# Moving the merging of norm statistics and small per-row operations from VectorE to GpSimd in a four-layer graph network kernel

## Chip, cores and metric

The kernel runs as one program on one NeuronCore of a Trainium2 chip. The metric is the device time of one execution in microseconds (us). The core has five engines with their own instruction queues, each served in order: PE (TensorE, matrix multiplication; PEld is its weight load), DVE (VectorE), ACT (ScalarE), POOL (GpSimd) and SP (SyncE, which here only issues DMAs). They meet through semaphores alone, so the order in each queue is fixed when the program is built.

## The reference

There are 32 graphs of 512 nodes with 64 features, with a weighted adjacency matrix (some 1.6% of the entries by chance, on a symmetric pattern, and all diagonals) and a node mask. Four layers follow each other, and each ends in a norm over the 64 features of a node:

```python
def _layernorm(x, axis=-1, eps=1e-5):
    m = jnp.mean(x, axis=axis, keepdims=True)
    v = jnp.var(x, axis=axis, keepdims=True)
    return (x - m) / jnp.sqrt(v + eps)

x = _layernorm(x + _L0_gnn_ref(x, adj), axis=-1)   # degree-normalised sum over neighbours
x = _layernorm(x + _L1_gnn_ref(x, adj, ...), axis=-1)   # Chebyshev polynomials of the Laplacian, 4 orders
x = _layernorm(x + _L2_gnn_ref(x, adj, ...), axis=-1)   # hyperbolic attention over all pairs of nodes
x = _layernorm(x + _L3_gnn_ref(x, adj, nodemask, ...), axis=-1)   # weighted quantiles over the neighbours, two dense layers
return x
```

Layer 2 forms for all pairs of nodes a logarithmic map, an attention weight and a weighted sum, and then an exponential map back. Layer 3 thins out the neighbours of busy nodes, sorts each feature over a node's neighbours and mixes the quartiles.

## The kernel before

A graph of 512 nodes is held as T = 4 tiles of 128 partitions, so a value for each node is a tile of 128x4 (`col`) and a feature matrix one of 128x256 (`wide`). For each of the 32 graphs (batches) five stages are written down, called lanes: *front* (load the adjacency blocks, transpose them, layers 0 and 1), *pairs* and *tail* (layer 2), *graph* (which neighbours remain, the order of the nodes, the slots), *gather* and *sort* (layer 3: one-hot matmuls bring neighbour features into slots, a network of max and min sorts them), and for every two batches *head* (the rest of layer 3, the dense layers and the last norm). The last two batches use the lane *ends* for some of head's work, and *check* tests the node degrees against the limits of the fast path. A dense path for other graphs stands behind a branch (`tc.If`) and isn't taken on these data.

None of this is issued in the order in which it is written. Class `Order` (lines 181 to 400) is a recorder: helpers such as `tt`, `ts`, `stt` (DVE, lines 447 to 455), `act` (ACT, 477), `gtt` and `gts` (POOL, 470 to 475) and `mm` (PE) don't issue but record an operation with its engine, an assumed issue time, an assumed further delay until its result can be read (tail), and what it reads and writes. `issue` (line 295) then plays all of it through on five assumed clocks. An operation becomes ready when what it depends on is done by these times (another engine's result costs HOP = 0.1 us more, DVE's a further 0.15). Of the ready operations of an engine, the one with the smallest due time is taken; a due time is a period of 80 us times the batch number plus a share between the two bounds that the table `STAGES` gives the lane (line 1415). On PE, an operation of another tile shape than the last is set back by `STAY` us (line 188). Gaps of PE that the recorder sees are filled with matmuls on zeros (`stay_active`, lines 1453 and 1454; 1081 of them), and a change between ACT's two tables of functions puts in a table load. The resulting order is then pinned for each engine.

So a recorded time does two things: it says where an operation comes in the order, and where its readers do. The time on the chip is another matter; an engine waits there for whatever its next instruction in order needs.

The norms are made by `layernorm` (line 725), four times a batch: two in front (on `z`, and on layer 1's sum in PSUM into `FL`), one in tail (into `x3`) and one in the dense part of head (in place on `zo`). Each takes four statistics on DVE (line 714: `bn_stats` leaves six columns for each tile, count, mean and variance times count, of the even and of the odd elements), merges them with four `bn_aggr` (line 717, into `mv`), adds epsilon (`var`, DVE), takes the power -0.5 on POOL (`rsqrt`, line 722), makes the offset -mean times that (`off`, DVE), and applies both on ACT. The second front norm's caller reads the variance again.

Other small operations that the change touches: in front the degree `deg` gives `dm`, its power `dsc` and a mask `pos` (all 128x4); in graph `order` copies the rank to `rkh`, which head reads much later; in tail `s1` is put together from two columns and a row sum. POOL also clears parts of the sort's buffers SB and SH (line 1157), for which it waits until the sort of an earlier batch has let go of them.

Of the kernel before, what the change touches and what calls it, by code (L numbers as in the profile page):

```python
# [8 lines left out]
F32 = mybir.dt.float32  # L9
# [11 lines left out]
P = 128  # L21
# [159 lines left out]
class Order:  # L181
# [3 lines left out]

    ENGINES = ("PE", "DVE", "ACT", "POOL", "SP")
    HOP = 0.1
    STAY = 51.0

    def __init__(self, nc, tc):  # L190
        self.nc, self.tc = nc, tc
# [212 lines left out]
def tile_adj_resnorm(ctx: ExitStack, tc: tile.TileContext, x, adj, nodemask, w1k, b1k, att_w, att_b,  # L404
# [42 lines left out]
    def tt(out, a, b, op):  # L447
        vec(lambda: nc.vector.tensor_tensor(out, a, b, op=op), out, [a, b])  # L448

    def ts(out, a, s1, s2, op0, op1=None):  # L450
        kw = {} if op1 is None else {"op1": op1}
        vec(lambda: nc.vector.tensor_scalar(out, a, s1, s2, op0=op0, **kw), out, [a], True, (s1, s2))  # L452
# [4 lines left out]
    def cp(out, a):  # L457
        vec(lambda: nc.vector.tensor_copy(out, a), out, [a], True)
# [6 lines left out]

    def gp(f, out, ins):

        seq.op("POOL", 1.0, 0.5, f, [out], ins)

    def gtt(out, a, b, op):  # L470
        gp(lambda: nc.gpsimd.tensor_tensor(out, a, b, op=op), out, [a, b])
# [247 lines left out]
    def rsqrt(v, name):  # L719

        y = col(name)
        seq.op("POOL", 0.8, 0.6, lambda: nc.gpsimd.tensor_tensor(y, v, mhalf, op=OP.pow), [y], [v])  # L722
        return y

    def layernorm(dst, z):

        st = seq.tile(pools["small"], [P, T, nc.vector.BN_STATS_DIM], F32, "st", 2)
        mv = seq.tile(pools["small"], [P, T, nc.vector.BN_AGGR_DIM], F32, "mv", 2)
        for t in range(T):
            bn_stats(st[:, t, :], z[:, t, :])  # L730
        for t in range(T):
            bn_aggr(mv[:, t, :], st[:, t, :])
        var = col("var")
        ts(var, mv[:, :, 1], EPS, None, op0=OP.add)
        rs = rsqrt(var, "rs")
        off = col("off")
        stt(off, mv[:, :, 0], -1.0, rs, op0=OP.mult, op1=OP.mult)
        for t in range(T):
            act(dst[:, t, :], z[:, t, :], AF.Identity, bias=off[:, t:t + 1], scale=rs[:, t:t + 1])
        return mv[:, :, 1], rs  # L740
# [89 lines left out]
    def order(b, res):  # L830

        gm = pools["gm"]
        V = res["V"]
        key = col("key")
        stt(key, M3[:, b, :], float(N), iotr, op0=OP.mult, op1=OP.add)
        pt = bank()
        for t in range(T):
            tr(pt[:, t * P:(t + 1) * P], key[:, t:t + 1].to_broadcast([P, P]), identf)
        keyh = col("keyh")
        ts(keyh, key, -0.5, None, op0=OP.add)  # L840
        sg = col("sg")
        for t in range(T):
            junk = seq.tile(gm, [P, N], F16, "junk", 1)
            act(junk, pt, AF.Sign, bias=keyh[:, t:t + 1], scale=-1.0, accum_out=sg[:, t:t + 1])
        rk = col("rk")
        ts(rk, sg, -0.5, 0.5 * N - 1.0, op0=OP.mult, op1=OP.add)

        rkh = seq.tile(pools["keep"], [P, T], F16, "rkh", 8)
        cp(rkh, rk)
        perm = seq.tile(gm, [P, T, N], F16, "perm", 1, "nbT")  # L850
        for t in range(T):
            ts(perm[:, t, :], iotap, rk[:, t:t + 1], None, op0=OP.is_equal)
        VP = seq.tile(gm, [P, T, N], F16, "VP", 1, "v")
        for j in range(T):
            pt = bank()
            for t in range(T):
                mm(pt, V[:, t, j * P:(j + 1) * P], perm[:, t, :], start=(t == 0), stop=(t == T - 1))
            act(VP[:, j, :], pt, AF.Copy)
        slot = seq.tile(pools["keep"], [P, T, N], F16, "slot", 2)
        for j in range(T):  # L860
            pt = bank()
            for k in range(j + 1):
                mm(pt, UC[:, :P] if k == j else UC[:, P:2 * P], VP[:, k, :], start=(k == 0), stop=(k == j))
            act(slot[:, j, :], pt, AF.Copy)
        pt = bank()
        for k in range(T):
            mm(pt, onesP, VP[:, k, :], start=(k == 0), stop=(k == T - 1))
        if b % 2 == 0:
            res["ohm"] = OHM[:, b // 2 % 3]
        dist = seq.tile(gm, [P, H2], F16, "dist")  # L870
        for i in range(P // HM):
            hm, h = slice(i * HM, (i + 1) * HM), i % 2
            act(dist[hm], pt[hm, h * H2:(h + 1) * H2], AF.Abs, bias=npart[hm])
        for i, hm in enumerate((PADS, RANKS)):
            act(res["ohm"][hm, i, b % 2, :], dist[hm], AF.Relu, bias=1.0, scale=-1.0)
        res["slots"] = slot, rkh
# [5 lines left out]
    def front(b, res):  # L882

        A, xa = load(b)
        mid = pools["mid"]
        AT = transposed(A)
        res["AT"] = AT

        def amul(rhs, n):

            pt = bank()[:, :T * n].rearrange("p (t n) -> p t n", n=n)
            for t in range(T):
                for j in range(T):
                    mm(pt[:, t, :], AT[:, j, t * P:(t + 1) * P], rhs[:, j, :],
                                     start=(j == 0), stop=(j == T - 1))
            return pt

        def amul_halves(y):

            pt = bank()  # L900
            for j in range(2):
                for h in range(2):
                    mm(pt[h * D:(h + 1) * D, :], y[:, 2 * h + j, :], AT[:, 2 * h + j, :], start=(j == 0), stop=(j == 1), pair=True)
            sums = seq.tile(mid, [P, N], F32, "sums", 1)
            act(sums, pt, AF.Copy)
            pt = bank()[:, :T * D].rearrange("p (t n) -> p t n", n=D)
            for t in range(T):
                mm(pt[:, t, :], sums[:, t * P:(t + 1) * P], fold, start=True, stop=True)
            return pt


        pt = amul(xa, D + 1)
        deg = col("deg")
        cp(deg, pt[:, :, D])
        dc = col("dc")
        ts(dc, deg, 1.0, None, op0=OP.max)
        recip(dc, dc)
        z = wide("z")
        tt(z, pt[:, :, :D], bc(dc), op=OP.mult)
        tt(z, z, xa[:, :, :D], op=OP.add)  # L920
        R = seq.tile(mid, [P, T, KO * D], F32, "R", 1)
        layernorm(R[:, :, :D], z)


        dm = col("dm")
        ts(dm, deg, 2e-35, None, op0=OP.max)
        dsc = rsqrt(dm, "dsc")
        pos = col("pos")
        ts(pos, deg, 0.0, None, op0=OP.is_gt)
        tt(dsc, dsc, pos, op=OP.mult)  # L930
        g = col("g")
        ts(g, deg, 0.0, None, op0=OP.not_equal)
        for k in range(1, KO):
            prev = R[:, :, (k - 1) * D:k * D]
            y = wide("y")
            tt(y, prev, bc(dsc), op=OP.mult)
            pt = amul_halves(y)
            q = wide("q", "y")
            tt(q, pt, bc(dsc), op=OP.mult)
            cur = R[:, :, k * D:(k + 1) * D]  # L940
            if k == 1:
                pg = wide("pg", "z")
                tt(pg, prev, bc(g), op=OP.mult)
                prev = pg
            tt(cur, prev, q, op=OP.subtract)
        RT = seq.tile(mid, [P, KO * D // P, N], F32, "RT", 1)
        for u in range(KO * D // P):
            pt = bank()
            for t in range(T):
                tr(pt[:, t * P:(t + 1) * P], R[:, t, u * P:(u + 1) * P], identf)  # L950
            act(RT[:, u, :], pt, AF.Copy)
        pt = bank()[:, :T * (D + 2)].rearrange("p (t n) -> p t n", n=D + 2)
        nu = KO * D // P
        for t in range(T):
            mm(pt[:, t, :], onesb, bias1, start=True, stop=False)
            for u in range(nu):
                mm(pt[:, t, :], RT[:, u, t * P:(t + 1) * P], wk[:, u, :], start=False, stop=(u == nu - 1))

        FL = FLS[:, b % 2]
        var, rs = layernorm(FL[:, :, :D], pt[:, :, :D])  # L960
        tt(FL[:, :, D + 2:D + 7:4], pt[:, :, D:], bc(rs, 2), op=OP.mult)

        w2 = col("w2")
        stt(w2, var, float(D), rs, op0=OP.mult, op1=OP.mult)
        tt(FL[:, :, D:D + 34:33], bc(w2, 2), bc(rs, 2), op=OP.mult)
        ts(FL[:, :, D + 3:D + 36:32], bc(FL[:, :, D], 2), -1.0, 1.0, op0=OP.mult, op1=OP.add)
        res["FL"] = FL

    def pairs(b, res):
# [126 lines left out]
        s1 = col("s1")  # L1096
        gtt(s1, SS[:, :, D], SS[:, :, D + 1], op=OP.add)
        q = rowsum(x2, S, "xs")
        stt(s1, q, -2.0, s1, op0=OP.mult, op1=OP.add)
        tt(s1, s1, hh, op=OP.mult)  # L1100
        u = wide("u")
        tt(u, S, bc(hb), op=OP.mult)
        v = wide("v")
# [280 lines left out]
    def within_bounds():  # L1384
# [17 lines left out]
        for i, op in enumerate((OP.is_gt, OP.is_lt)):  # L1402
# [9 lines left out]

    STAGES = {"front": (-0.6, -0.5), "pairs": (1.2, 1.3), "tail": (0.2, 1.5), "graph": (0.9, 1.0), "gather": (2.7, 2.9),
              "sort": (4.5, 4.6), "head": (4.7, 5.6), "ends": (4.0, 4.5), "check": (3.4, 4.8)}

    nc.scalar.preload_act_table_set("natural_log_exp_and_others")
    with ExitStack() as fast:
# [285 lines left out]
```

## Time and profile before

| What | Value |
|---|---|
| Runs | 2621.48, 2621.71, 2628.53 us, median 2621.71 |
| The profiled execution | 2622.02 us, its span 2620.2 us, mean granted PE clock 0.982 |
| Busy, DVE / PE / ACT / POOL | 2402.7 / 2458.2 / 1879.2 / 815.8 us |
| Largest DVE groups | SB products (sort) 565.8 us, SH products 347.4 us, one-hots `oh` 252.3 us |
| The power on POOL, front norms | 64 times, mean 1303 ns, 83.4 us |
| Aggregations `bn_aggr` | front 256 times, 33.5 us; head 128, 11.7 us; tail 128, 11.5 us |
| DMA | 49.96 MB in the span, mean 19 GB/s |

The span goes from the first to the last instruction of the profiled execution. A group is named by the program's tiles, output <- inputs, with the lane ahead (`tail_mv<-tail_st`), and its shapes. Busy time is the time in which at least one instruction of the group or engine ran; instructions of DVE overlap with the next one, so that 128 aggregations of 148 ns (median) are busy for 11.5 us only. A wait is the time in which an engine's next instruction stood idle, with the instruction that released it. In the timeline a line gives the start in us from the span's start, the length, and how many like it follow each other. The slices of the page are 65.5 us long.

### The profile page before, as it was taken

To read this page: it belongs to the slowest core of one execution; us is meant where nothing else is said; L and a number is where in the kernel's file an instruction comes from. 1 tells how busy PE (TensorE), PEld (TensorE's weight loads), DVE (VectorE), ACT (ScalarE), POOL (GpSimd) and SP (SyncE) were. 2 spreads that over 40 slices of the span, in tenths; PEclk is the share of its full clock that TensorE was granted. 3 is DMA by queue.
4 is the path that set the end of the run, shared out by engine and by line. 5 is a ranking of instruction groups with operands and counts; after the bars stand their busy time and mean duration, and the time that the engine had idled before them with its cause. 6 is when DMAs were issued, how large, how long until landed. Compare 5 with 4: busy or idle time off the path is not lost.

```text
span 2620.2 us, 55667 instructions
## 1 busy us (share of the span) xinstructions
PE 2458.2 (94%) x19641; PEld 1635.4 (62%) x19667; DVE 2402.7 (92%) x9002; ACT 1879.2 (72%) x4406; POOL 815.8 (31%) x1783
## 2 busy tenths in 40 slices
PE   7999999999999999999999999999999999999997
PEld 6666566666666666666656666566666666666655
DVE  3668998999999999999999999999999999998996
ACT  5666677767777777767777677777777778776761
POOL 1233332332343333322333233333323333332210
PEclk9999999999999999999999899999999999998999
DMA  1100000000000000000000000000000000000000
GB/s 38 33 23 21 17 14 15 25 22 23 18 11 22 20 25 21 24 17 13 20 21 25 19 19 13 20 23 22 26 19 13 18 19 26 19 11 3 5 7 8
DMA packets 119723, 49.96 MB, mean 19 GB/s; under 512 B 53740, under 2 KB 119436, under 8 KB 119436
## 3 DMA queue, kind: packets, MB, share of 16 engines
q1 hardware_dynamic: 118272, 46.15, 6.4%
q8 instruction: 156, 2.56, 0.4%
q14 instruction: 131, 1.07, 0.1%
q10 hardware_dynamic: 1164, 0.18, 0.0%
HBM read 37.93 MB, written 8.39 MB: 18 GB/s over the span
## 4 chain that ended last, share of the span: by engine, by line
DVE 72%; PE 18%; ACT 6%; issue 2%; POOL 2%; DMA 0%; ACTq 0%; DVEq 0%
DVE SB L448 17%; DVE SH L448 8%; DVE gather_oh L452 6%; PE front_bank L502 5%; DVE pairs_Q L448 4%; PE gather_bank L502 3%; PE graph_bank L502 3%; DVE pairs_RW L448 3%; PE pairs_bank L502 3%; DVE sort_prod L448 3%; DVE pairs_Wt L455 3%; DVE pairs_L L455 2%; DVE tail_v L448 2%; DVE pairs_EX L448 2%; DVE pairs_RW L455 2%
## 5 line engine op out<-in xcount | busy, mean ns | idle before, releaser
L448 DVE TENSOR_TENSOR SB<-SB 128x448 f32<-128x448 f32 (+11 forms) x1424 | 565.8, 424 | 12.2 <-ACT SB L483 0.7
L502 PE MATMUL gather_bank<-gather_oh,tail_x3h 128*64 128x448 f16 (+5 forms) x5376 | 516.5, 321 | 4.8 <-ACT SB L483 3.4
L502 PEld LDWEIGHTS <-tail_x3h 128*64 128x64 bf16 x5376 | 296.0, 111 | 214.3 <-issue 112.8
L448 DVE TENSOR_TENSOR SH<-SH 128x32 f32<-128x32 f32 (+11 forms) x1744 | 347.4, 246 | 8.1
L502 PE MATMUL pairs_bank<-pairs_FT 67*128 67x512 f32 (+7 forms) x768 | 316.9, 516 | 18.7 <-ACT pairs_EX L483 7.1
L452 DVE TENSOR_SCALAR gather_oh<-graph_slot 128x256 f16<-128x256 f16 (+9 forms) x864 | 252.3, 337 | 25.3 <-PE gather_bank L502 23.5
L502 PE MATMUL front_bank<-front_AT,front_y 128*64 128x512 f32 x768 | 189.5, 607 | 18.5 <-DVE front_y L448 17.0
L502 PEld LDWEIGHTS pairs_bank<-pairs_FT 67*128 67x128 f32 (+1 forms) x768 | 130.2, 194 | 83.2 <-issue 19.7
L502 PE MATMUL graph_bank<-graph_perm,graph_V 128*128 128x512 f16 x512 | 141.0, 382 | 16.1 <-DVE graph_perm L452 13.8
L502 PEld LDWEIGHTS <-graph_nbT 128*128 128x128 f16 x1536 | 113.1, 99 | 57.6 <-issue 17.3
L722 POOL TENSOR_TENSOR front_rs<-front_var,mhalf 128x4 f32<-128x4 f32 x64 | 83.4, 1303 | 201.8 <-DVE front_var L452 152.9
L502 PEld LDWEIGHTS front_bank<-XA,front_AT 128*128 128x128 f32 x1024 | 126.0, 194 | 13.6 <-issue 6.3
L1453 PE MATMUL PA<-zero 128*128 128x256 bf16 x973 | 132.9, 278 | 0.1
L502 PE MATMUL pairs_bank<-FLS,pairs_Wt 128*128 128x66 f32 x1024 | 124.7, 274 | 3.9 <-DVE pairs_Wt L455 3.8
L502 PEld LDWEIGHTS pairs_bank<-FLS,pairs_Wt 128*128 128x128 f32 x1024 | 120.6, 192 | 10.9 <-DVE pairs_Wt L455 7.8
L502 PE MATMUL front_bank<-XA,front_AT 128*128 128x65 f32 x1024 | 124.5, 274 | 0.0
L448 DVE TENSOR_TENSOR pairs_RW<-pairs_RW,pairs_EX 128x640 f32<-128x640 f32 x128 | 104.1, 815 | 18.7 <-ACT pairs_RW L483 18.4
L502 PEld LDWEIGHTS <-tabs 128*128 128x128 f16 x1296 | 78.3, 100 | 64.2 <-issue 54.9
L502 PEld LDWEIGHTS front_bank<-front_AT,front_y 128*64 128x64 f32 x768 | 54.5, 137 | 95.6 <-issue 63.0
L483 ACT ACTIVATE graph_VP<-graph_bank 128x512 f16<-128x512 f32 x128 | 75.5, 590 | 53.7 <-PE graph_bank L502 49.4
L483 ACT ACTIVATE SB<-gather_bank 128x448 f32<-128x448 f32 (+2 forms) x192 | 81.3, 438 | 43.4 <-PE gather_bank L502 43.0
L502 PE MATMUL head_bank<-head_PT,sort_ap 128*64 128x512 f32 x240 | 111.2, 608 | 0.1
(354 smaller groups left out, 6569.8 us busy)
## 6 DMA issues: line engine op xcount, KB each, us to landing
front_A<-in_adj_dram SPq DMA_DIRECT2D x128, 256.0 KB, 2.7
XA<-in_x_dram SPq DMA_DIRECT2D x32, 128.0 KB, 2.2
xs<-tail_x SPq DMA_DIRECT2D x32, 128.0 KB, 1.9
out_dram<-head_zo SPq DMA_DIRECT2D x31, 128.0 KB, 2.0
out_dram<-tail_ends SPq DMA_DIRECT2D x1, 128.0 KB, 2.1
wk<-in_L_gnn_weight_dram ACTq DMA_DIRECT2D x1, 64.0 KB, 3.0
w1s<-in_L_gnn_W_dram ACTq DMA_DIRECT2D x2, 32.0 KB, 2.0
attw<-in_L_gnn_att_W_dram ACTq DMA_DIRECT2D x2, 0.2 KB, 3.2
```

Of the source, the lines that this page charges most:

```text
L448: vec(lambda: nc.vector.tensor_tensor(out, a, b, op=op), out, [a, b])
L452: vec(lambda: nc.vector.tensor_scalar(out, a, s1, s2, op0=op0, **kw), out, [a], True, (s1, s2))
L455: vec(lambda: nc.vector.scalar_tensor_tensor(out, a, s, b, op0=op0, op1=op1), out, [a, b], False, (s,))
L483: 0.3, lambda: nc.scalar.activation(out, a, f, scale=scale, **kw), [out, accum_out], [a, after] + sc, table)
L502: return nc.tensor.matmul(out, w, a, start=start, stop=stop)
L722: seq.op("POOL", 0.8, 0.6, lambda: nc.gpsimd.tensor_tensor(y, v, mhalf, op=OP.pow), [y], [v])
L1453: return nc.tensor.matmul(PA[:, 2 * P:], zero[:, :P], zero, start=False, stop=False)
```

## The change

- `layernorm` gets a parameter `soon`. The two front norms pass True and stay as they were. For the two others (tail and head) the merging of the statistics is written out for POOL: the mean of the means, the squared half difference of the means, the sum of the variances divided by 64, the power, and the offset. The statistics themselves stay on DVE and the last step on ACT.
- Six further operations on 128x4 move from DVE to POOL: `dm`, `pos` and the product with `dsc` in front, the copy `rkh` in graph, and in tail the two steps on `s1` (which become three).
- The recorder's assumed times for POOL go from 1.0 + 0.5 us to 0.28 + 0.25 for a small operation and from 0.8 + 0.6 to 1.1 + 0.3 for the power; `STAY` goes from 51 to 49, and in `STAGES` the bounds of tail, graph, gather, ends and check are altered. These four change the order on every engine.

```diff
-    STAY = 51.0
+    STAY = 49.0
...
-        seq.op("POOL", 1.0, 0.5, f, [out], ins)
+        seq.op("POOL", 0.28, 0.25, f, [out], ins)
...
-        seq.op("POOL", 0.8, 0.6, lambda: nc.gpsimd.tensor_tensor(y, v, mhalf, op=OP.pow), [y], [v])
+        seq.op("POOL", 1.1, 0.3, lambda: nc.gpsimd.tensor_tensor(y, v, mhalf, op=OP.pow), [y], [v])
...
-    def layernorm(dst, z):
+    def layernorm(dst, z, soon=False):
+
+        if not soon:
+
+            st = seq.tile(pools["small"], [P, T, nc.vector.BN_STATS_DIM], F32, "st", 2)
+            for t in range(T):
+                bn_stats(st[:, t, :], z[:, t, :])
+            off, even, var, d, odd, v = (st[:, :, i] for i in range(6))
+            gtt(d, even, odd, op=OP.subtract)
+            gtt(var, var, v, op=OP.add)
+            gts(d, d, 0.5, None, op0=OP.mult)
+            gts(var, var, 1.0 / D, EPS, op0=OP.mult, op1=OP.add)
+            gtt(d, d, d, op=OP.mult)
+            gtt(v, var, d, op=OP.add)
+            rs = rsqrt(v, "rs")
+            gtt(off, even, odd, op=OP.add)
+            gts(off, off, -0.5, None, op0=OP.mult)
+            gtt(off, off, rs, op=OP.mult)
+            for t in range(T):
+                act(dst[:, t, :], z[:, t, :], AF.Identity, bias=off[:, t:t + 1], scale=rs[:, t:t + 1])
+            return
...
-        cp(rkh, rk)
+        gts(rkh, rk, 1.0, None, op0=OP.mult)
...
-        layernorm(R[:, :, :D], z)
+        layernorm(R[:, :, :D], z, True)
...
-        ts(dm, deg, 2e-35, None, op0=OP.max)
+        gts(dm, deg, 2e-35, None, op0=OP.max)
         dsc = rsqrt(dm, "dsc")
         pos = col("pos")
-        ts(pos, deg, 0.0, None, op0=OP.is_gt)
-        tt(dsc, dsc, pos, op=OP.mult)
+        gts(pos, deg, 0.0, None, op0=OP.is_gt)
+        gtt(dsc, dsc, pos, op=OP.mult)
...
-        var, rs = layernorm(FL[:, :, :D], pt[:, :, :D])
+        var, rs = layernorm(FL[:, :, :D], pt[:, :, :D], True)
...
-        stt(s1, q, -2.0, s1, op0=OP.mult, op1=OP.add)
-        tt(s1, s1, hh, op=OP.mult)
+        gts(q, q, -2.0, None, op0=OP.mult)
+        gtt(s1, s1, q, op=OP.add)
+        gtt(s1, s1, hh, op=OP.mult)
...
-    STAGES = {"front": (-0.6, -0.5), "pairs": (1.2, 1.3), "tail": (0.2, 1.5), "graph": (0.9, 1.0), "gather": (2.7, 2.9),
-              "sort": (4.5, 4.6), "head": (4.7, 5.6), "ends": (4.0, 4.5), "check": (3.4, 4.8)}
+    STAGES = {"front": (-0.6, -0.5), "pairs": (1.2, 1.3), "tail": (0.7, 1.2), "graph": (1.2, 1.3), "gather": (2.7, 3.1),
+              "sort": (4.5, 4.6), "head": (4.7, 5.6), "ends": (4.3, 4.4), "check": (3.4, 4.7)}
```

## The prediction

> **What bounds the kernel now.** I read the page first, then the busy time by stretches, then DVE's waits, then DVE's timeline inside one batch. From the page:
>
> ```profile
> PE 2458.2 (94%) x19641; PEld 1635.4 (62%) x19667; DVE 2402.7 (92%) x9002; ACT 1879.2 (72%) x4406; POOL 815.8 (31%) x1783
> DVE  3668998999999999999999999999999999998996
> DVE 72%; PE 18%; ACT 6%; issue 2%; POOL 2%; DMA 0%; ACTq 0%; DVEq 0%
> ```
>
> DVE is busy 92% of the span, in slices four to thirty-nine nearly always, and 72% of the chain that ended last is DVE. PE's 94% is no proof of a bound, since its matmul ends are modelled and it holds filler matmuls (line 1453). POOL, the engine that takes the work over, is busy 31%.
>
> The steady stretch, first all engines, then the fillers alone (columns: stretch, length, busy time of PE, PEld, DVE, ACT, POOL, PE clock, DMA share, GB/s; in the second line only PE and PEld):
>
> ```profile
> 656.00:2296.00 1640.00, 1558.03 (x12419) 1025.93 (x12436) 1569.64 (x5852) 1237.58 (x2905) 548.38 (x1135) 0.99 0.07 20
> ```
>
> ```profile
> 656.00:2296.00 1640.00, 22.26 (x138) 12.88 (x138) 0.99 0.07 20
> ```
>
> DVE is busy 95.7% here, and PE without the fillers 1558.0 - 22.3 = 1535.8 us, 93.6%. So DVE is the tighter of two engines that are nearly level. DVE idles 70 us here, of which its waits on PE and ACT for operands are most; its waits on POOL in the whole run are:
>
> ```profile
> DVE head_off L455 <- POOL head_rs L722: 4.0, 5, 1.1
> DVE front_off L455 <- POOL front_rs L722: 3.4, 5, 0.9
> DVE tail_off L455 <- POOL tail_rs L722: 1.7, 3, 0.9
> ```
>
> (us in total, number of times, longest). 9.1 us over 128 places (64 + 32 + 32): 0.07 us a place. That matters below, because these three are the places where the recorder's old time for POOL (0.8 + 0.6 us for the power, line 722) was already close to the measured 1.3 to 1.5 us.
>
> **What the change takes off DVE.** Per batch: two norms (tail and head) lose four aggregations, one variance and one offset each (12 instructions); six more go to POOL (dm, pos, the product with dsc, the copy rkh, two on s1). That is 18 of 128x4 or less, 576 over 32 batches; the built lists agree. What one is worth is read from the timeline, as the distance to the next start and not as its length, since neighbours overlap:
>
> ```profile
> 1379.38 0.36 DVE L717 BATCH_NORM_AGGREGATE head_mv<-head_st 128x2 f32<-128x6 f32 x4
> 1379.66 0.19 DVE L452 TENSOR_SCALAR gather_oh<-graph_slot 128x256 f16<-128x256 f16 x1
> 1379.78 0.17 DVE L452 TENSOR_SCALAR head_var<-head_mv 128x4 f32<-128x4 f32 x1
> 1379.86 0.49 DVE L452 TENSOR_SCALAR gather_oh<-graph_slot 128x256 f16<-128x256 f16 x3
> ...
> 1384.23 0.15 DVE L455 SCALAR_TENSOR_TENSOR tail_off<-tail_mv,tail_rs 128x4 f32<-128x4 f32 x1
> 1384.31 1.08 DVE L448 TENSOR_TENSOR SB<-SB 128x896 f32<-128x896 f32 x1
> ```
>
> Four aggregations hold DVE for 0.28 us, a variance for 0.08, an offset for 0.08. So two norms: 2 x (0.28 + 0.08 + 0.08) = 0.88 us. The other six at the same 0.07 (dm at 1425.09, pos at 1425.16, the next at 1425.23; rkh at 1413.72, the next at 1413.80): 0.42. Together 1.3 us a batch, **-41 us** over 32. If each counted its busy time in the group rows, it would be 11.7 + 11.5 for the aggregations and some 50 for the ten others, 73 us: the far end. The near end is zero, if DVE only idles longer. I take -41, because the starts are what a full queue is made of.
>
> The two offsets also take their waits off DVE: 4.0 + 1.7, **-6 us**.
>
> **What it adds.** POOL gets 25 instructions a batch (9 for each of two norms, 3 for dsc, 1 for rkh, 3 for s1), 800 in all. Rows of the same shape take 0.25 to 0.45 us in most groups (tail_al<-tail_xy 247 ns, pairs_sq 461 ns): some 270 us, so POOL goes from 816 to about 1090 us, 42%. Hidden beside DVE, if its answers come in time. Where are they awaited? The power that it delays is no longer followed by DVE in tail and head but by ACT, which has 28% idle. On DVE there are six places a batch that read a POOL answer and that the recorder used to plan too late (1.0 + 0.5 us an operation) and now plans at 0.28 + 0.25: two reciprocals, the products with s1, al, y2 and rnr. Planned closely, a place costs what the three above cost: 6 x 32 x 0.07 = **+14 us**. Bounds: zero (nothing late), and for the far end the row with the widest spread: tail_nr 769 ns, the power 1421, tail_rnr 762, 2.95 us in sequence against 0.53 + 1.4 + 0.53 = 2.46 now planned, 0.5 us late, 6 x 32 x 0.5 = 96 us.
>
> POOL is served in order, and a fill of SB (line 1157) waits there for DVE:
>
> ```profile
> POOL SB L1157 <- DVE SB L448: 263.6, 65, 17.9
> ```
>
> 65 waits, up to 17.9 us. Behind a fill the built order has a power of the front norm 26 times (18 before), and the new s1 steps 12 times. A front power that stands there is late for DVE's front_off. The row front_off (3.4 us) is what 18 such places cost in the worst reading; 26 add under 2 us, which lies inside the +14.
>
> End of the run: the last two norms stand alone. Now aggregation to offset takes 2611.64 to 2614.51. Then eight small POOL steps come ahead of each power and one product after it; undisturbed ones start every 0.15 to 0.35 us in the trace. Two norms in one queue: 18 x 0.25 = 4.5 us, less 0.9 us of aggregation and variance and 0.3 of the two offsets: **+3 us**.
>
> ACT gets 125 table loads in place of 109; one takes 1283 ns, 16 make 20.5 us. ACT is 6% of the chain, so **+1 us**; all 20 if ACT were late everywhere. Fillers go from 1081 to 932 on PE: nothing, they stand where PE has no work.
>
> Sum: -41 - 6 + 14 + 3 + 1 = -29. From the profiled execution's 2622.0 us (span 2620.2 and 1.8 around it; it lies 0.3 above the median of the runs, 2621.7, which changes nothing): **2593 us**. The altered shares of the pipeline (graph, tail and ends later or narrower) I cost at nothing: summed over the built orders with this trace's distances, the DVE work ahead of the last one-hot of the first gather is 101 us before and 99 after the change, that behind the last front 230 and 220, some of which are removed instructions themselves.
>
> **A rule that speaks against it.** A row first: SB products of 128x448 take the same with POOL at work beside them (1392.94, with pairs_two on POOL) as with POOL idle (1391.37), 0.61 us both, while POOL's own small ones stretch from 0.20 to 0.55 there. The Trainium skill, SBUF — State Buffer, section "Who interferes with whom", has it that VectorE and GpSimd share a port pair as an exclusive lock, and that a VectorE instruction with two SBUF inputs and a GpSimd instruction that reads SBUF block each other, whoever comes second waiting in full. By that rule 800 more GpSimd instructions could hold DVE for up to their 270 us and the kernel would be near 2850. In the trace only POOL is seen to stretch, so I count nothing for it.
>
> **Rivals.**
> 1. *PE takes the bound.* After the change DVE needs 1569.6 - 21.5 x 1.3 = 1542 us of the steady stretch (21.5 batches of 76 us), PE 1536. Level, each waits for the other, and half of the 41 us comes back as idle time. For it: 93.6% of real PE work. Against: the PE waits of this stretch name DVE (front_st 15.8, front_y 10.8, graph_perm 8.3 us), which gets faster. 2593 + 15 = 2608, with a spread of 2600 to 2614.
> 2. *The closer plan fits better than I count.* If the recorder's order, freed of POOL steps that it took for three times as long, also closes a third of DVE's 70 idle us, 23 us more: 2570, down to 2550 if the removed instructions are worth their whole 73.
> 3. *POOL's answers come late (slower).* Place: the six DVE places, and front_off behind the merges and the fills. Price: up to the 0.5 us of the rnr row each, +96 in place of +14: 2593 + 82 = 2675. It decides from 47 / 192 = 0.25 us a place on, where 47 us of gain are spent. For it: POOL instructions of up to 4 us in the trace (tail_nr 4.12 on the chain), and DVE's instructions are fixed in order, so one late answer holds all behind it. Against: the 0.07 us of the closely planned places of today.
> 4. *No difference:* DVE's freed time returns wholly as waits for gather_bank, pairs_RW and front_st (23.5, 18.4, 17.1 us now): 2615 to 2628.
>
> **How the numbers follow.** Forecast (2578 to 2600) 0.42; rival 1, 0.20; rival 2, 0.16; rival 4, 0.08; rival 3, 0.14. Less than 0.3%, 7.9 us, a measurement of this kernel can't tell from no change; so faster is under 2613.8: 0.42 + 0.20 + 0.16 less a little of rival 1's upper edge, 0.77. Same 0.09, slower 0.14. The range leaves out rival 3's upper part and the far low end: 2555 to 2632.
>
> **What would show it.** DVE busy near 2403 - 41 = 2362 us (2330 if full lengths count), with 9002 - 576 = 8426 instructions; DVE's share of the steady stretch still 95% or more. DVE waits on POOL: no head_off or tail_off, and al, y2, s1, rnr and the reciprocals together some 14 us; 60 us there is rival 3. PE's real share over 95% with new DVE waits on PE is rival 1. POOL near 1090 us with 2583 instructions, ACT near 1900. If DVE's SB products of 128x448 lengthen over 617 ns, the port rule has been right and I wrong. I am also wrong if the fill of the pipeline (first 328 us, DVE busy 230.5) or the drain (the last 160 us, 136.7) changes by more than 10 us, which I set at nothing.

## The result, and the profile after

The changed kernel takes **2669.09 us** (median of 4 runs, 2665.76 to 2670.40) against 2624.84 for the kernel before in the same comparison: ratio **1.0166 [1.0146, 1.0187]**, 1.7% slower. The forecast was 2593, and the range ended at 2632. The profiled execution took 2670.4 us, 48 more than that of before.

From the page of the changed kernel, the lines that answer to those shown of before:

```profile
PE 2489.6 (93%) x19518; PEld 1636.8 (61%) x19518; DVE 2377.7 (89%) x8426; ACT 1892.7 (71%) x4422; POOL 1025.9 (38%) x2583
DVE  3568999899899989999999998999999889998996
```

DVE has 576 instructions fewer and is busy 25 us less, yet idles 291 us (2668.6 - 2377.7) where it idled 217.5. (The chain of waits tells nothing this time: it is followed back over a few steps only.) The steady stretch, all engines, then the fillers of the main line alone (1473 here, 1453 before):

```profile
656.00:2296.00 1640.00, 1549.76 (x12139) 1008.03 (x12140) 1521.81 (x5400) 1211.54 (x2844) 672.21 (x1630) 0.97 0.07 19
```

```profile
656.00:2296.00 1640.00, 12.33 (x80) 7.52 (x80) 0.97 0.07 19
```

PE without fillers is busy 1549.8 - 12.3 = 1537.4 us, as before (1535.8), but for 12059 matmuls in place of 12281. The same kind of work took PE 127.5 ns a matmul instead of 125.1, 2% more, and the column ahead of the DMA share says why: the granted clock is 0.97 where it was 0.99. **A busy share of PE counts the time at half clock as work**, so 93% and 94% looked alike while PE got less done. Over the whole span:

```profile
core 0: 2668.6 us, clock 0.966
```

Before it was 0.982. The missing part of the clock is 0.034 x 2668.6 = 91 us against 0.018 x 2620.2 = 47. The trace's record of the granted clock knows two values, full and half: 25 stretches at half speed, 184.5 us together, against 14 and 97.0 before.

DVE's waits (total us, number, longest), first the largest and then those on POOL:

```profile
DVE tail_rem L448 <- ACT tail_x3h L483: 39.3, 28, 3.9
DVE pairs_EX L455 <- PE pairs_bank L502: 35.0, 16, 6.2
...
DVE gather_oh L452 <- PE gather_bank L502: 15.0, 13, 3.5
...
DVE pairs_dn L461 <- POOL pairs_dn L475: 4.6, 6, 1.6
...
DVE front_off L455 <- POOL front_rs L722: 2.4, 4, 1.1
...
DVE tail_v L448 <- POOL tail_al L471: 0.9, 2, 0.6
```

The places that the prediction watched wait on POOL for under 10 us in all. The new line is the first one, and it names ACT, not POOL. The tile tail_x3h holds layer 2's normed result as a sum of three bf16 parts: ACT makes the first from tail_x, and DVE's tail_rem, the remainder, needs it. Before, all that touches tail_x3h waited 4.9 us for ACT together. (pairs_EX, second in the list, waited 9.3 us before. It can't be the main cause: with the tail norm alone on POOL, below, the loss is as large and this line 11.7 us.) ACT's own waits lead on, first of the changed kernel, then of before:

```profile
ACT tail_x L483 <- POOL tail_st L471: 49.2, 23, 5.0
ACT head_zo L483 <- POOL head_st L471: 33.8, 11, 11.4
```

```profile
ACT tail_x L483 <- DVE tail_off L455: 35.5, 23, 3.8
ACT head_zo L483 <- DVE head_off L455: 25.1, 17, 6.2
```

**One batch, from engine to engine.** DVE's timeline first (start, length, what, how many, idle time before):

```profile
2418.55 0.60 DVE L714 BATCH_NORM_STATS2 tail_st<-tail_v 128x6 f32<-128x64 f32 x4
...
2419.48 0.82 DVE L448 TENSOR_TENSOR pairs_RW<-pairs_RW,pairs_EX 128x640 f32<-128x640 f32 x1
2420.21 1.56 DVE L455 SCALAR_TENSOR_TENSOR pairs_RW<-pairs_RW 128x640 f32<-128x640 f32 x2
2421.68 1.56 DVE L448 TENSOR_TENSOR pairs_EX<-pairs_EX,pairs_RW 128x640 f32<-128x640 f32 x2
...
2430.20 0.42 DVE L448 TENSOR_TENSOR tail_rem<-tail_x,tail_x3h 128x256 f32<-128x256 f32 x1 [3.88 <-ACT tail_x3h L483]
```

The same time on POOL:

```profile
2419.24 5.18 POOL L471 TENSOR_TENSOR tail_st<-tail_st 128x4 f32<-128x4 f32 x3 [3.54 <-DVE tail_st L714]
2424.50 1.38 POOL L475 TENSOR_SCALAR tail_st<-tail_st 128x4 f32<-128x4 f32 x3
2425.84 0.55 POOL L471 TENSOR_TENSOR tail_st<-tail_st 128x4 f32<-128x4 f32 x2
2426.47 1.03 POOL L722 TENSOR_TENSOR tail_rs<-tail_st,mhalf 128x4 f32<-128x4 f32 x1
```

and on ACT:

```profile
2427.81 1.43 ACT L483 ACTIVATE tail_x<-tail_v,tail_st,tail_rs 128x64 f32<-128x64 f32 x4 [3.56 <-POOL tail_st L471]
2429.27 0.47 ACT L483 ACTIVATE graph_dist<-graph_bank,npart 32x256 f16<-32x256 f32 x1
2429.76 0.42 ACT L483 ACTIVATE tail_x3h<-tail_x 128x256 bf16<-128x256 f32 x1
```

The statistics are there at 2419.1. POOL's first three small steps take 5.18 us, while DVE multiplies 128x640 tiles beside them, and the power starts 7.3 us after the statistics; the recorder had planned about 3.1 (eight steps of 0.28, twice 0.25 of tail, 0.34 to get from DVE to POOL). On the mean of the 32 batches the power starts 4.6 us after the statistics. ACT, which serves its queue in order, stands 3.56 us before tail_x. Behind it wait graph_dist, which PE needs, and tail_x3h, which DVE's tail_rem needs, so DVE stands 3.88 us, and PE too. Three windows of this moment (stretch, length, busy time of PE, PEld, DVE, ACT, POOL, PE clock, DMA share, GB/s):

```profile
2418.00:2427.60 9.60, 9.58 (x71) 4.95 (x69) 8.29 (x21) 3.21 (x7) 7.89 (x10) 1.00 0.01 2
2427.60:2431.50 3.90, 0.54 (x17) 0.58 (x17) 0.42 (x1) 3.57 (x10) 0.17 (x1) 1.00 0.15 34
2431.50:2434.90 3.40, 3.39 (x22) 2.46 (x23) 2.27 (x10) 3.40 (x7) 0.00 (x0) 0.50 0.00 0
```

For 3.9 us PE and DVE do almost nothing, and for the next 3.4 PE runs at half clock. The Trainium skill, TensorE: Matmul & The Clock Gate, Part 1, states such a gate: after an idle window of about 3.4 us PE's clock is halved. The moment above agrees: 0.54 us of work in 3.90, then 0.50. So does the length: all half-speed stretches but the last are multiples of 3.41 us (3.4 to 17.1). But as a rule for this kernel it is too mild. In the 3.41 us just ahead of each of the 25 half-speed stretches PE was busy for 0.13 to 2.95 us, and before, ahead of the 14, for 1.55 to 2.97: a stretch far from idle was enough here. A gap that the recorder foresees holds filler matmuls; this one it did not foresee.

### The profile page after: what moved, and what is told of

It reads as the page before. It is cut to its first block, busy times and chain, and to the rows that moved or that the text cites. A ratio compares the mean times of both kernels' runs of the same rounds, so it can differ in the third digit from the quotient of the medians.

```text
span 2668.6 us, 55676 instructions
## 1 busy us (share of the span) xinstructions
PE 2489.6 (93%) x19518; PEld 1636.8 (61%) x19518; DVE 2377.7 (89%) x8426; ACT 1892.7 (71%) x4422; POOL 1025.9 (38%) x2583
## 5 line engine op out<-in xcount | busy, mean ns | idle before, releaser
L502 PE MATMUL gather_bank<-gather_oh,tail_x3h 128*64 128x448 f16 (+5 forms) x5376 | 545.4, 325 | 8.3 <-ACT SB L483 4.2
L448 DVE TENSOR_TENSOR SH<-SH 128x32 f32<-128x32 f32 (+10 forms) x1744 | 346.8, 246 | 8.0
L502 PE MATMUL pairs_bank<-pairs_FT 67*128 67x512 f32 (+7 forms) x768 | 322.3, 527 | 11.2 <-DVE pairs_EX L455 6.2
L502 PEld LDWEIGHTS pairs_bank<-pairs_FT 67*128 67x128 f32 (+1 forms) x768 | 136.9, 199 | 86.8 <-issue 33.8
L722 POOL TENSOR_TENSOR front_rs<-front_var,mhalf 128x4 f32<-128x4 f32 x64 | 77.9, 1218 | 267.8 <-DVE front_var L452 236.8
L502 PEld LDWEIGHTS front_bank<-XA,front_AT 128*128 128x128 f32 x1024 | 134.9, 205 | 17.5 <-issue 11.0
L1177 POOL MEMSET SB<- 128x10 f32 (+2 forms) x96 | 12.5, 132 | 343.0 <-DVE SB L448 329.2
L483 ACT ACTIVATE graph_v<-graph_bank,graph_c 128x512 f16<-128x512 f32 x128 | 87.9, 687 | 72.4 <-PE graph_bank L502 63.3
L502 PE MATMUL front_bank<-XA,front_AT 128*128 128x65 f32 x1024 | 134.0, 286 | 0.0
L471 POOL TENSOR_TENSOR tail_st<-tail_st 128x4 f32<-128x4 f32 x160 | 91.7, 593 | 108.6 <-DVE tail_st L714 106.1
```

The source lines that it names most:

```text
L483: 0.3, lambda: nc.scalar.activation(out, a, f, scale=scale, **kw), [out, accum_out], [a, after] + sc, table)
L502: return nc.tensor.matmul(out, w, a, start=start, stop=stop)
L722: seq.op("POOL", 1.1, 0.3, lambda: nc.gpsimd.tensor_tensor(y, v, mhalf, op=OP.pow), [y], [v])
L1177: seq.op("POOL", 0.3, 0.3, lambda d=d: nc.gpsimd.memset(d, PAD), [d], [])
```

## The experiments

The expectations name theories by letters. On the loss:

- A: POOL's merge in the tail norm comes later than planned, and ACT hands that on to DVE and PE. In one form only the lateness against the pinned order counts, in another the delay itself ("pure delay").
- B: the recorder's short times for POOL make an order that is too tight everywhere.
- C: the altered shares and `STAY` cost it.
- D: any merge on POOL costs alike, by load and contention there.

On what relief of DVE is worth: E, DVE and PE are level, and each takes back what the other gains; F, DVE alone bounds; or DVE's relief was never worth 41 us. G: any change makes the recorder draw a new order, and the old shares fit the old order alone. Ratios stand against the kernel before, run beside each kernel.

### Which part carries the loss

**Merging on DVE again**, all else as changed:

```diff
-    def layernorm(dst, z, soon=False):
+    def layernorm(dst, z, soon=True):
```

> The changed kernel with all four norms merged on DVE again; moved small operations, recorder times and shares stay as changed. Theory A (the tail norm's merge on POOL answers late: last statistics to first apply 6.6 us on average in place of 3.2, so that ACT waits 49 us for tail_st and DVE 39 us for tail_x3h): most of the 45 us comes back, 2625 to 2640. Theory B (the recorder's close POOL times make an order that is too tight everywhere): stays above 2655. Theory C (the altered shares and STAY): stays above 2655.

2629.02 us, 1.0014 [0.9985, 1.0044]. The loss is gone with the merge, though six small operations a batch stay on POOL and times and shares are the new ones. B and C, which had expected more than 2655, fall as the cause of these 45 us.

**Only the head norm on POOL** (tail's call gets `True`), and **only the tail norm** (head's call gets `True`):

> The changed kernel with the tail norm merged on DVE again; only the head norm is merged on POOL. Theory A (the tail norm's merge comes later than the order allows, and DVE's and PE's next work on x3 stands behind it): 2605 to 2630, no wait of tail_rem. Rival D (any merge on POOL costs alike, by load on POOL): about half of the 42 us over the variant without merges, 2645 to 2655.

> The changed kernel with the head norm merged on DVE again; only the tail norm is merged on POOL. A: 2655 to 2675, with the wait of tail_rem for tail_x3h still 30 us or more. D: 2645 to 2655.

Head only: 2622.54 us, 1.0008 [0.9991, 1.0025]. Tail only: 2670.13 us, 1.0188 [1.0149, 1.0228]. DVE's wait for tail_x3h, head only and then tail only:

```profile
DVE tail_rem L448 <- ACT tail_x3h L483: 2.9, 3, 1.4
```

```profile
DVE tail_rem L448 <- ACT tail_x3h L483: 36.0, 35, 4.3
```

The tail norm carries the whole loss, as A expected; the head norm's merge on POOL costs nothing. There ACT's wait at head_zo is 33.4 us, 23 of them in the last 70 us of the run (before, 25.1 for head_off); in the kernel nothing but the output is made from this result.

**The load without the wait**: merging on DVE, and nine POOL steps for each tail and head norm on a tile that nobody reads:

```diff
+            jk = seq.tile(pools["small"], [P, T], F32, "jk", 1)
+            gtt(jk, even, odd, op=OP.subtract)
...
+            gtt(jk, jk, jk, op=OP.mult)
```

> The variant with all norms merged on DVE (2629), and beside them nine POOL steps for each tail and head norm, read from the same statistics, whose results nobody uses. So POOL has the changed kernel's load, and no norm waits for it any longer than the queue makes it. D (load and contention): 2660 or more. A: 2625 to 2645, the part over 2629 being the power that stands behind some of the idle steps.

2618.45 us, 0.9982 [0.9960, 1.0004], with POOL busy 1023.5 us as in the changed kernel. D falls: 576 unused POOL steps cost no time that shows. (The time lies a little under what A had expected.)

**The merge priced as it runs**: only the recorder's times for the steps on `st` change.

```diff
-        seq.op("POOL", 0.28, 0.25, f, [out], ins)
+        slow = out.tensor.name.split("_")[1:2] == ["st"]
+        seq.op("POOL", 0.45 if slow else 0.28, 0.35 if slow else 0.25, f, [out], ins)
```

> The changed kernel; only the recorder's time for the merge steps goes from 0.28 + 0.25 to 0.45 + 0.35 us, about what they take on the chip. A as lateness against the order: the order now puts other work ahead of tail_rem, its wait falls under 15 us and the time to 2600 to 2635. A as pure delay, or D: 2655 to 2685.

2622.33 us, 0.9998 [0.9975, 1.0022]. Same instructions; from the last statistics to ACT's first apply it still takes 6.9 us on the mean of the 32 batches (3.2 before, 6.6 in the changed kernel), but now other work stands in the queues between:

```profile
DVE tail_rem L448 <- ACT tail_x3h L484: 5.9, 10, 1.4
```

ACT's wait for the merge falls from 49.2 to 15.8 us, PE's gaps of over 1 us after the first 100 us from 39 (69 us) to 26 (34 us; before 27 and 37; PE here with its weight loads). This is A's strongest support. It isn't the delay alone that costs, since the delay is still there; but any new price also draws the whole order anew. All kernels with the tail merge on POOL and the full work on PE, those of the next section too, show whether tail_rem's wait follows lateness against the plan. Planned is the sum from above with each kernel's times (for 1.0 + 0.5: 8 x 1.0 + 2 x 0.5 + 0.34), measured the mean of 32 batches, both in us from the last statistics to the start of the power:

| Kernel | planned | measured | wait of tail_rem |
|---|---|---|---|
| changed | 3.1 | 4.6 | 39.3 |
| tail norm only | 3.1 | 4.5 | 36.0 |
| changed, old `STAGES` and `STAY` | 3.1 | 4.5 | 29.5 |
| all small POOL steps at 0.37 + 0.3 | 3.9 | 4.0 | 9.0 |
| merge at 0.45 + 0.35 | 4.6 | 4.2 | 5.9 |
| before, norms merged on POOL, old times | 9.3 | 7.7 | 8.1 |
| changed, old POOL times | 9.3 | 7.7 | 8.2 |

Where the merge comes 1.4 us or more later than planned, tail_rem waits 30 us and more; where it comes about as planned or earlier, under 10, though in the last two rows the delay itself is longest.

**All small POOL steps at 0.37 + 0.3**:

> The changed kernel with the recorder's time for every small POOL operation at 0.37 + 0.30 us, the mean from one start to the next in the trace, in place of 0.28 + 0.25. If lateness against the order is the cause, this mends it without singling out the merge: 2605 to 2635, tail_rem's wait under 15 us. If the singled-out price was a lucky order: above 2650.

2632.79 us, 1.0061 [1.0039, 1.0084], tail_rem 9.0 us. Most of the loss is gone; pricing only the slow chain does better.

### The other parts alone, and what an order is worth

Each of these undoes or does one part, and each redraws the order of every queue. The last column is the number of filler matmuls in the built order, which is the recorder's own picture of PE's holes (1081 before, 932 in the changed kernel).

| Kernel | us | ratio | fillers |
|---|---|---|---|
| changed, old POOL times (1.0 + 0.5, power 0.8 + 0.6) | 2715.47 | 1.0325 [1.0272, 1.0378] | 1785 |
| changed, old `STAGES` and `STAY` | 2686.64 | 1.0217 [1.0163, 1.0271] | 1199 |
| before, tail and head norms merged on POOL | 2688.31 | 1.0228 [1.0171, 1.0284] | 1612 |
| before, the six small operations on POOL | 2663.46 | 1.0190 [1.0156, 1.0224] | 1549 |
| before, new POOL times | 2664.03 | 1.0183 [1.0148, 1.0218] | 1263 |
| before, new `STAGES` and `STAY` 49 | 2626.34 | 1.0044 [1.0022, 1.0066] | 1096 |
| before, `STAY` 53 | 2663.77 | 1.0191 [1.0169, 1.0213] | 1345 |

In the order of the table:

> The changed kernel with the recorder's old times for POOL (1.0 + 0.5 and 0.8 + 0.6 us); norms and small operations stay on POOL, shares as changed. A: the recorder now allows the merge some 10 us, so DVE's order leaves room and tail_rem no longer waits: 2600 to 2630. B: 2590 to 2620, too. C: above 2655. If the merge's delay itself is what costs, whatever the order: above 2660.

> The changed kernel with the old table of shares and STAY 51. C: 2585 to 2625. A and B: 2660 to 2680, nothing comes back.

> The kernel before with only the tail and head norms merged on POOL; old recorder times, old shares, small operations on DVE. A as lateness against the order: the old times leave room, DVE has 28 us less to do, 2595 to 2620. A as pure delay: 2640 or more. B and C: 2595 to 2620, since neither of their parts is in it.

> The kernel before with only the six small operations moved to POOL; old times and shares. Relief counts: 13 us less (192 DVE operations), less what the recorder, which takes POOL for slow, puts later: -15 to +5 us. If the recorder's view of a slow POOL is what costs: 10 us or more longer.

> The kernel before with only the recorder's new POOL times. No work is moved. If the closer plan costs by late answers on DVE (the six places of the prediction): 10 to 30 us longer. If it is harmless: within 8 us.

> The kernel before with only the new shares and STAY 49. As costed in the prediction: within 8 us. If the shares by themselves eat the relief: 15 us or more longer.

> The kernel before with nothing but STAY 53 in place of 51: no operation is added, moved or priced otherwise, only the order is drawn anew. The recorder sees more holes on PE in it, 1345 fillers in place of 1081. Theory G (any change makes the recorder draw a new order, and the old shares fit the old order alone; an order with many fillers is a bad one, as in all slow variants but the changed kernel and the one with the tail merge alone): 2645 to 2675. If the order is drawn anew without harm: within 10 us of before.

The last one is the lesson:

```diff
-    STAY = 51.0
+    STAY = 53.0
```

It adds and moves no operation of the program and costs 46 us, as much as the whole change. DVE's wait for gather_bank shows the worse order:

```profile
DVE gather_oh L452 <- PE gather_bank L502: 57.3, 35, 3.9
```

23.5 before, 15.0 in the changed kernel, 42 to 53 in the other rows over 1.018 of the table. So most of these rows measure a new order and not the part that they are named after. That holds for A too: with the old times (first and third row) it had expected 2600 to 2630 and 2595 to 2620, its form of pure delay above 2660 and 2640. The times fit the latter, but tail_rem waits only 8 us there, and gather_bank 48 and 46, so they don't decide between the two.

A new order isn't free of work either. With `STAY` 53 the fillers on PE are busy for 187 us in place of 147. Between 100 and 2400 us they stand in 137 runs (99 us), and after 97 of these (72 us) PE's next matmul follows within 0.1 us; before, after 69 of 95 (46 of 63 us). There the fillers may have held it up. Whether the 46 us come from the fillers or from the holes that they stand for was not tested.

What the rows do show: new shares without the rest cost little, and no part of the change pays alone. Of the kernels with their full work on PE, those with up to 1100 fillers run at 2614 to 2633 us; the two exceptions are the changed kernel and its tail-norm-only form (1025), where the loss is not a hole that the recorder saw but an answer that came late. Those with 1199 and more run at 2645 to 2715.

### What relief of DVE is worth

**More on DVE**: nine small operations after each tail and head norm, on a tile that nobody reads.

```diff
+            jk = seq.tile(pools["small"], [P, T], F32, "jk", 1)
+            for _ in range(9):
+                ts(jk, mv[:, :, 1], 1.0, None, op0=OP.mult)
```

> The kernel before with 18 more DVE operations of 128x4 a batch (nine after the tail norm, nine after the head norm, results unused), 576 in all, as many as the change takes away. F: 35 to 45 us longer, 2655 to 2670. E: 15 to 35 us longer. If 576 small operations are worth nothing in either direction: under 10 us.

2692.96 us, 1.0283 [1.0249, 1.0318]. Longer than any theory had expected, and inconclusive: the built order has 1500 fillers. The probes themselves took about what was intended, though their rows look like twice that:

```profile
L452 DVE TENSOR_SCALAR head_jk<-head_mv 128x4 f32<-128x4 f32 x288 | 47.1, 164 | 0.5
L452 DVE TENSOR_SCALAR tail_jk<-tail_mv 128x4 f32<-128x4 f32 x288 | 45.9, 160 | 0.0
```

The rows sum up whole lengths, 93 us, most of which lie beside the neighbours of other groups. By the distance to the next start, the price used in the prediction, the 576 hold DVE for 48 us (0.07 each in the median), and DVE's busy time grew by 47 (2402.7 to 2449.6).

**Fifteen small operations a batch less** (in tail and head the power and the last step take the statistics of the even elements alone, and the degree loses its guard and its mask), with the times and shares of before and, second, with the new times, shares and `STAY` 49:

```diff
+            mean, var = st[:, :, 1], st[:, :, 2]
+            rs = rsqrt(var, "rs")
...
-        ts(dm, deg, 2e-35, None, op0=OP.max)
-        dsc = rsqrt(dm, "dsc")
-        pos = col("pos")
-        ts(pos, deg, 0.0, None, op0=OP.is_gt)
-        tt(dsc, dsc, pos, op=OP.mult)
+        dsc = rsqrt(deg, "dsc")
```

> The kernel before, old recorder times and shares, with 15 small DVE operations a batch left out and none put on POOL: in the tail and head norms the aggregation, the variance and the offset (the power and the last step take two raw columns of the statistics), in front dm, pos and the product with dsc. 480 operations, 35 us by the distances of their starts. If DVE's relief counts as such: 25 to 45 us less than before. If something else holds the pace: within 10 us of before.

> The 15 small DVE operations a batch left out as in the relief variant, but with the changed kernel's recorder times, shares and STAY, which give 980 fillers in place of 1217. The norms of tail and head have no aggregation, variance and offset, front has no dm, pos and product with dsc. If DVE's relief counts once the order fits: 2575 to 2605. If it is worth nothing in any order: 2612 to 2632, like all variants with few fillers so far.

First 2645.13 us, 1.0110 [1.0079, 1.0141]: taking work away made it slower, with 53.1 us at gather_bank and 1217 fillers. Second 2614.50 us, 0.9983 [0.9964, 1.0002], with 980 fillers and nothing added to POOL:

```profile
656.00:2296.00 1640.00, 1557.02 (x12370) 1024.30 (x12387) 1553.59 (x5525) 1236.86 (x2902) 518.15 (x1135) 0.98 0.07 20
```

DVE is at 94.7% here instead of 95.7, PE where it was. So relief that should by my price be worth some 35 us (15 of the 18 instructions) gave 3, with an interval that takes in zero. That supports the rival that DVE's relief was never worth 41 us. It doesn't show it, since orders with few fillers differ by some 18 us among themselves, but none of those with relief came out below 2614.

**Less on PE**: the gather's third bf16 part is left out, in the kernel before and in the kernel with the merge priced.

```diff
-                    for q in range(3):
+                    for q in range(2):
```

> The kernel before without the third bf16 part of the gathered features: 1792 of 5376 gather matmuls are left out (the values are less exact), some 170 us of PE work by the 96 ns each of the group row. DVE's work stays. Theory E (DVE and PE are level, each takes back what the other gains): 2540 to 2600. Theory F (DVE alone bounds): 2610 to 2625. PE alone bounds: under 2500.

> The changed kernel with the priced merge, without the third bf16 part. E: with PE out of the way the 41 us of DVE's relief show, so 25 to 45 us less than the same cut in the kernel before. If ACT, latencies or the order swallow the relief: within 12 us of it.

2566.07 us, 0.9806 [0.9769, 0.9843], and 2572.11 us, 0.9820 [0.9779, 0.9861]. PE relief pays at once, even with some 1500 fillers in both orders, but less than a third of the 170 us that were taken off. Theory E had 2540 to 2600 for the first. But with PE relieved, DVE's relief still gave nothing; that was expected to pay by then if PE alone held the pace, and stays unexplained.

### The clock

The executions of one kernel differ in granted clock, and their time goes with it: over 192 executions of all kernels here, each against the mean of its own kernel and group, a clock lower by 0.01 went with 0.68% more time (correlation -0.94). Lengths on DVE and ACT don't follow the clock (ACT's pairs_RW of 128x640 takes 732 ns in both kernels). If the clock were the cause, PE would hold the end for about two thirds of the time; but a stall that lengthens an execution can also lower its clock, and which of the two leads is not shown. By the same slope the 1.6 points from 0.982 to 0.966 are worth about 1.1%, 29 of the 48 us between the profiled executions; the rest would be the stalls themselves, an estimate that takes the clock for the cause. It isn't the only way to lose: the kernel with the tail norm alone on POOL had 0.977 and took 2657.4 us, and the one with only the six operations moved had 0.987 in its profile and took 2657.9 us.

## Why the prediction was wrong

- **The failed step**: "The power that it delays is no longer followed by DVE in tail and head but by ACT, which has 28% idle." I priced ACT's lateness at nothing by its idle share. But ACT's queue is in order, and right behind tail_x stand graph_dist, for PE, and tail_x3h, for DVE's tail_rem. Of the 128 norms only the 32 in tail matter: 39.3 us of DVE's waits hang on them, and without their merge on POOL the 45 us are gone. Of the lost clock, 91 us instead of 47, only a part is theirs: with the tail norm alone on POOL it is 61 us. With it, "Rows of the same shape take 0.25 to 0.45 us" was too kind: the tail merge's steps are the worst placed on POOL,

```profile
L471 POOL TENSOR_TENSOR tail_st<-tail_st 128x4 f32<-128x4 f32 x160 | 91.7, 593 | 108.6 <-DVE tail_st L714 106.1
```

  and take 593 ns on the mean against 327 for the same steps in head. DVE's long pairs products run just then: 40 of the 160 ran mostly beside products of 128x640 and took 57 of the 95 us. So the power started 4.6 us after the statistics where the order had been drawn for 3.1.
- **Rival 3** named the kind (late answers of POOL, in fixed queues) and, by chance, nearly the time (2675), but the wrong place: the six DVE places and front_off. There the sum held: +14 forecast (6 x 32 x 0.07 is 13.4), under 10 us measured. My sign that "60 us there is rival 3" would have cleared it wrongly.
- **-41 us** failed as well. The instructions went as counted (9002 to 8426), DVE's busy time fell by 25 us, and a like relief in a level order gave 3 us. "So DVE is the tighter of two engines that are nearly level" was read from 95.7% against 93.6%; the 48 us from less PE work say that PE sets a part of the pace. Rival 1 saw this and still left the change a gain of 14 us. Even with the merge well priced, the change is worth nothing (0.9998).
- **-6 us**: head_off and tail_off are gone from DVE's waits, but ACT took the wait over: 49.2 us on POOL's tail_st where it had waited 35.5 us for DVE's tail_off. In head, too: 33.8 on POOL's head_st, 25.1 on head_off before. The sum should have followed it there.
- **+3 us at the end**: right. From the first statistics of the last two norms to the end of ACT's last line it is 8.85 us (2656.08 to 2664.93) where it was 5.87 (2610.62 to 2616.49).
- **Altered shares at nothing**: nearly right for their total (2626.34 alone, 1.0044 [1.0022, 1.0066]), wrong as a method. Summed DVE work ahead of the first gather can't see what an order is worth; a tie-break moved by 2 us costs 46. Fill and drain changed by less than the 10 us allowed (first 328 us: DVE 230.5 to 221.6; last 160 us: 136.7 to 130.8). The loss is in the pace: from the fifth front to the last they follow each other every 78.8 us instead of 77.2.
- **Fillers at nothing**: "they stand where PE has no work" is true of the recorder's clocks. On the chip, before the change, PE's next matmul follows within 0.1 us after 69 of 95 runs of fillers between 100 and 2400 us, so some may have been in its way. What a filler costs or saves was not measured alone.
- **Port rule at nothing**: right for DVE, whose SB products are as long as before (617 ns then):

```profile
L448 DVE TENSOR_TENSOR SB<-SB 128x448 f32<-128x448 f32 x352 | 217.0, 618 | 3.4
```

  Counted for DVE only, though; that POOL's own steps stretch, which I saw in the trace, is what made the merge late.

**What stays open.** What exactly holds the pace near 77 us a batch: PE's share is supported by the run with less PE work, and the clock goes with it, but the pair with less PE work and less DVE work speaks against PE alone. How the loss divides between stalls and clock is an estimate. A late merge in an otherwise unchanged order was not tried, nor were orders with their fillers left out. No version with its full work on PE beat both kernels beyond its interval; the closest was the unused POOL load (0.9982 [0.9960, 1.0004]), which is less than one order differs from another.

## What to carry to other kernels

When an operation moves to another engine, follow its answer through every in-order queue to the engines that hold the end, and price each step at what it takes beside the work that runs at that moment, not at the mean row; an idle share of the engine in between hides nothing from those queued behind the wait. Where a recorder draws the order from assumed times, measure first what a neutral redraw costs, and compare parts only between orders with equally few holes. A busy share of PE must be read together with its granted clock.

## What the runs showed of the hardware

- Small steps on POOL depend on DVE's neighbour work far more than I had thought: the TENSOR_TENSOR steps of the tail merge, all 128x4, take 199 ns at least, 272 in the median and 4873 at most. Beside DVE's products of 128x640 they take 0.8 to 2.1 us on the mean (by group), beside front_q, of which one input lies in PSUM, 0.20. DVE's own products don't lengthen (128x448: 617 and 618 ns; 128x640: 815 and 817). The Trainium skill, SBUF — State Buffer, "Who interferes with whom", lets whoever comes second wait in full; in these traces only POOL is seen to pay.
- One late answer can cost twice: the gap itself, and then PE at half clock for 3.4 us or more. Of the 11 waits of tail_rem over 1 us, six have a half-speed stretch that begins within 3 us of them. PE need not have been idle for 3.4 us: 1.55 to 2.97 us of work in the 3.41 us ahead didn't keep the clock up in the kernel before.
- A small DVE operation that follows another one onto the very same tile starts later: 0.20 us after it in all 15 places of the probes where that happens, against 0.07 to 0.08 where the next one writes elsewhere.
